# A four-layer hybrid kernel on one core: convolution pieces and the first step size issued ahead of the rest of the projection, and an L1 gate product that reads PSUM

## The chip, the core and the metric

The kernel is one program on one core of a Trainium2 chip. The engines named below are PE (matrix products, with PEld for its weight loads), DVE (vector), ACT (scalar functions), POOL (GpSimd) and SP, whose queue issues every DMA of this kernel. Each engine works through its own list of instructions in order. SBUF is the on-chip memory, PSUM the eight banks that PE writes to and that DVE and ACT can also read and write. The metric is device time in microseconds (us); lower is better. Each kernel is run several times and the median is taken, and one further execution is profiled.

## The reference, cut to what matters

The input x is [4, 96, 64, 64] in float32: batch, channels, height, width. Four layers follow; the change touches the first two.

Layer 0 is a selective scan over an image (d_inner 192, 16 states, 4 directions K):

```python
xz = layernorm(t) @ in_proj_w.T + in_proj_b
xi, z = jnp.split(xz, 2, axis=-1)                  # 192 channels each
xi = silu(depthwise_conv3x3(xi) + conv_b)          # per image [192, 64, 64]
xr = xi.reshape(b, 192, L)                         # row by row, L = 4096
xc = xi.transpose(0, 1, 3, 2).reshape(b, 192, L)   # column by column
xs = [xr, xc, flip(xr), flip(xc)]                  # the 4 directions
x_dbl = einsum('bkdl,kcd->bkcl', xs, x_proj_w)     # -> dts_r (6), B (16), C (16)
dt = softplus(einsum('bkrl,kdr->bkdl', dts_r, dt_projs_w) + dt_projs_b)
h = h * exp(dt * A) + dt * B * x ;  y = sum_n h * C   # step by step along L
y  = sum of the 4 directions + Ds * xs ;  layernorm ;  * silu(z) ;  @ out_proj_w.T
```

followed by a residual and a GELU MLP. Layer 1 is a smaller scan (96 channels, one state, 2 directions) whose last part is a layer norm, a gate and a product with a weight:

```python
y = (y - mu) * rsqrt(var + 1e-5)
y = y * out_norm_w + out_norm_b
y = y * silu(z)
out = einsum('oc,bchw->bohw', out_proj_w, y)
```

Layers 2 and 3 (a filter in the Fourier domain, a linear attention and two quantized MLPs) are not touched.

## The kernel before, in words

**A planner sets the order.** The parts of the kernel are Python generators, run as threads by the class `Work`. A thread yields `on(engine, events..., banks=n, took=..., table=...)` when it wants an engine, and the planner picks the thread whose request can start first by its own estimates of costs. The order in which instructions are issued comes out of that, once, when the program is built. Events (`post("rows", ...)`, `("begun",)`, ...) are conditions of this plan; data dependences are guarded apart from them. Lower `rank` wins between equals: the threads of the loop have 0 (`recurs` 2), those of the background 1. `par(jobs, n)` runs a list of jobs on n workers.

**The loop (layer 0's scan).** There are 64 steps, 16 for each batch b: directions k = 0, 1, 3, 2 with 4 chunks of 1024 positions. A step has 24 units (3 blocks j of channels, 4 groups q of states, 2 halves p). `preludes` prepares a step g on 512 columns and 128 partitions: it loads `xi`, multiplies it by `xw` (PE) and copies the result to `xd` (ACT), stores `bc`, then makes three products with `dtw` into banks, of which ACT takes Abs and Relu into `dtu`, then Exp and Ln over all three, then POOL adds and multiplies by `xi`; four puts store `dtu` to `dd` in DRAM. `loads_du` and `loads_bc` bring `u`, `dt`, `bb`, `cc` back, spread over 128 partitions, 512 KB each. For a unit, `decays` computes h = exp(A dt) into PSUM (ACT), `sources` w = u * bb (POOL), `recurs` the scan over h and w and then w = h * cc (DVE), and `gathers` sums w into `py` (PE). One unit in 12 has its last product on POOL (`side`). Buffers: 6 of w (`WB`), 3 of u and of dt (`DB`), 5 of bb and of cc (`RB`). `convolved` loads `xj`, the convolved input that opens a block's sum in direction 0.

**The front of layer 0.** `front(b)` has two phases. In `inproj(gp)`, four jobs that each take column group gp of both image halves: x is loaded and normalized, then multiplied by `w_in` three times: into `xp01` (channels 0 to 127, padded image), `xp2` (channels 128 to 191, the two image halves on two halves of the partitions), and `z`, of which ACT takes Silu before it is stored to `z_d`. Then come the convolutions: `conv(q)` for part 1 (from `xp2`, 4 pieces of 8 rows) and afterwards for part 0 (from `xp01`, 8 pieces), with three workers. A piece is 9 products with diagonal weights on PE, into a bank; for the first batch two pieces of each part are instead nine multiply-adds on DVE (`taps`), into the SBUF tile `xi` itself. ACT then takes Silu; POOL copies the piece, transposed, to `xt`; SP stores it to `xi_d`. After a part, `xt` is stored too: 2 puts for part 0, 16 for part 1, whose runs are 128 bytes.

**The start.** The program first runs `setup()` and `front(0)` with all eight banks (3 of `bm`, 5 of `bs`; `mode["wide"]`), until the event `("inproj", 0)`. Then the five `bs` banks are given to h and py, and the threads of the loop start; the convolutions of batch 0 run as background of the loop. Pieces of part 0 with q >= 2 wait for `("begun",)`, which step 0 posts after its Ln. After `front(0)` the background goes on with `prepare()` (weights for later layers, by many small loads), `front(1)` to `front(3)`, and `rest(b)` for the four batches: `tail`, `l1`, `l2_front`, `l2_middle`, `back`. A tail's four gates wait for the y of their chunk (`("y", b, c)`, c = 3, 2, 1, 0), which the loop stores as it finishes them in direction 2. When the loop is over, what is left of `rest(3)` runs alone, with eight banks again.

**The L1 gate.** In `l1`, `piece(n)` of the second direction ends with the normalization: `pv` is a bank that holds rsqrt of the variance, `dt` the centred y, `yf` the stored Silu(z). Two DVE instructions form the gated value in `a`, lines 928 to 931.

In the profile, most instructions carry the line of a helper: L227 is `mm` on PE, L242 `act` and L231 `copy` on ACT, L239 a table load of ACT, L254 an operation on DVE or POOL, L275 a load and L279 a store on SP. They are told apart by the names of their tiles.

Of the kernel before, what the change touches and what calls it, by code (L numbers as in the profile page):

```python
# [216 lines left out]
def tile_hybrid(ctx: ExitStack, tc: tile.TileContext, I: dict, out: bass.AP):  # L217
# [238 lines left out]
    def front(b):  # L456
# [3 lines left out]
        dgs = [px_.tile([128, 9, 128], F32, name=f"dg{i}") for i in range(2)]  # L460
        st, (wp, wk) = pools(bg("f1"), bg("f1w"))
# [23 lines left out]
        def inproj(gp):  # L485
            def job(t):
# [47 lines left out]
                ps = yield on("pe", banks=3)  # L534
# [17 lines left out]
        for i in range(2):  # L552
            get(dgs[i], I[("dg01", "dg2")[i]])
        yield from par([inproj(gp) for gp in range(4)], 2, 4)
        st.close()
# [3 lines left out]
        for part in (1, 0):  # L559
            rows = 64 if part == 0 else 32  # L560
            st, (wp, wk) = pools(bg(f"f2{part}"), bg(f"f2w{part}"))
            dg = dgs[part]
            xt = wp.tile([128, 64, rows], F32, name="xt")
            xp = (xp01, xp2)[part]

            def conv(q):
                def job(t):
                    xi = wt(wk, 128, "xi", t)
                    early = b == 0 and (t == 0 if part else q < 2)
                    if b == 0 and part == 0 and q >= 2:  # L570
                        yield on(None, ("begun",))
                    if early:
                        yield from taps(xi, xp, 8 * q, V("cw", j=9 * part, n=9))
                        pc = xi
                    else:
                        (pc,) = yield on("pe", banks=1)
                    for k in () if early else range(9):
                        kh, kw = divmod(k, 3)
                        r = 8 * q + kh
                        mm(  # L580
                            pc.rearrange("p (h w) -> p h w", w=WW), lhsT=dg[:, k, :],
                            rhs=xp[:, r : r + 8, kw : kw + 64], start=(k == 0), stop=(k == 8),
                        )
                        if k in (2, 5):
                            yield on("pe")
                    yield on("act", took=0.7, table=AF.Silu)
                    act(xi, pc, AF.Silu, bias=V("cb", j=part))
                    if not early:
                        drop(pc)
                    yield on("pool")  # L590
                    po_.tensor_copy(
                        xt[:, :, 8 * q : 8 * q + 8], xi.rearrange("p (h w) -> p w h", w=WW)
                    )
                    yield on("sp")
                    if part == 0:
                        put(xi_d[b][0, q, 0:128], xi)
                        post("rows", b, q, stored=True)
                    else:
                        for h in range(2):
                            put(xi_d[b][0, q + 4 * h, 128:192], xi[64 * h : 64 * h + 64])  # L600

                return job

            yield from par([conv(q) for q in range(rows // 8)], 3)
            if part == 1:
                post("half", b)
            yield on("sp")
            if part == 0:
                v = xi_d[b][1, :, 0:128, :].rearrange("g d t -> d g t")
                xf = xt.rearrange("p (g w) h -> p g (w h)", g=NG)  # L610
                for i in range(2):
                    put(v[:, 4 * i : 4 * i + 4], xf[:, 4 * i : 4 * i + 4])
            else:
                v = xi_d[b][1, :, 128:192, :].rearrange("g d (w h) -> d g w h", h=HH)
                for h in range(2):
                    for g in range(NG):
                        put(v[:, g, :, 32 * h : 32 * h + 32], xt[64 * h : 64 * h + 64, 8 * g : 8 * g + 8, :])
            st.close()
# [117 lines left out]
    def l1(b, stat, pp, big):  # L736
# [112 lines left out]
        def piece(n):  # L849
# [4 lines left out]
            def job(t):  # L854
# [73 lines left out]
                ve.scalar_tensor_tensor(a, dt, V("l1og", C), pv[0:C], ALU.mult, ALU.mult)  # L928
                drop(pv)
                yield on("dve")  # L930
                ve.scalar_tensor_tensor(a, a, V("l1ob", C), yf, ALU.add, ALU.mult)
# [431 lines left out]

    def preludes():
        ck, dp = fg["ck"], fg["dp"]
        for g, (b, k, s, c) in enumerate(steps):
            need = [("front", b)] if k % 2 else [("half", b), ("rows", b, 2 * c), ("rows", b, 2 * c + 1)]
# [29 lines left out]
            for j in range(3):  # L1397
                (pd,) = yield on("pe", banks=1)
                mm(pd, lhsT=dtw[:, j, :], rhs=xd[0:64], start=True, stop=True)
                yield on("act", took=1.3)  # L1400
                act(dtu[:, 0, j], pd, AF.Abs)
                act(dtu[:, 1, j], pd, AF.Relu)
                drop(pd)
            yield on("act", took=1.6, table=LN_EXP)
            act(dtu[:, 0], dtu[:, 0], AF.Exp, scale=-1.0)
            yield on("act", took=1.6, table=LN_EXP)
            act(dtu[:, 0], dtu[:, 0], AF.Ln, bias=one)
            if g == 0:
                post("begun")
            yield on("pool")  # L1410
            po_.tensor_add(dtu[:, 0], dtu[:, 0], dtu[:, 1])
            yield on("pool")
            po_.tensor_mul(dtu[:, 1], dtu[:, 0], xi)
            yield on("sp")
            dd = dp.tile([2, 3, 2, 32, 2, HC], F32, tag="dd", name="dd")
            for p in range(2):
                for hf in range(2):
                    r = p * 64 + hf * 32
                    put(
                        dd[:, :, p, :, hf, :].rearrange("t j d i -> d (t j) i"),  # L1420
                        dtu[r : r + 32].rearrange("d t j i -> d (t j) i"),
                    )
            sync()
            d["dd"] = dd
            post("dd", g)

    def loads_du():

        for n in range(6 * NS_):
            g, m = divmod(n, 6)  # L1430
            for t in (1, 0):
                need = [("dd", g)]
# [13 lines left out]
    def loads_bc():  # L1446

        for n in range(4 * NS_):
            g, q = divmod(n, 4)
            for t in range(2):  # L1450
                need = [("bc", g)]
                if n >= RB:
                    o, r = divmod(n - RB, 4)
                    need.append(("src" if t == 0 else "C", unit(o, 2, r, 1)))
                yield on("sp", *need)
                tag = ("bb", "cc")[t]
                x = fg["ring"].tile([128, CH], F32, tag=tag, name=tag)
                r = t * NS + 4 * q
                get(x, made[g]["bc"][r : r + 4].unsqueeze(0).to_broadcast([32, 4, CH]))
                made[g][tag, q] = x  # L1460
                post(tag, n)
                wk_.detach()
# [108 lines left out]
    def convolved():  # L1571

        was = None
        for block in range(3 * NS_):
# [4 lines left out]
            yield on("sp", ("half", b), ("rows", b, 2 * c + 1), ("bc", g), *([("xjf", was)] if was is not None else []))  # L1579
# [40 lines left out]
    with tc.manual_schedule():  # L1620
        stb = open_banks(3, "bm")
        st = open_banks(5, "bs")
        mode["wide"] = True
        first = wk_.add(setup()), wk_.add(front(0))
        wk_.run(lambda: first[0].done and ("inproj", 0) in wk_.events)
# [3 lines left out]
        st_sb, (ck, du, ring, wk, yp_, dp) = pools(  # L1629
# [192 lines left out]
```

## Time and profile before

Three runs took 6655.88, 6654.35 and 6673.25 us, median 6655.88. The profiled execution took 6648.81 us, of which 6647.0 lie between its first and last instruction (the span).

| stretch of the span, us | length | DVE busy | ACT busy | POOL busy | PE busy | what runs |
|---|---|---|---|---|---|---|
| 0 to 133.3 | 133.3 | 37.08 | 50.75 | 19.27 | 92.22 | setup, front(0), first prelude |
| 133.3 to 218 | 84.7 | 80.38 | 49.68 | 67.89 | 62.35 | step 0 |
| 218 to 251 | 33.0 | 17.24 | 10.78 | 18.43 | 13.49 | the passage to step 1 |
| 251 to 400 | 149.0 | 145.50 | 97.89 | 118.34 | 106.50 | steps 1 and 2 |
| 400 to 2000 | 1600.0 | 1469.15 | 1010.52 | 1277.86 | 1294.82 | loop, fronts, first rest |
| 2000 to 4000 | 2000.0 | 1887.86 | 1320.53 | 1592.93 | 1612.26 | loop and rests |
| 4000 to 5980 | 1980.0 | 1872.27 | 1402.35 | 1582.79 | 1576.59 | loop and rests |
| 6100 to 6647 | 547.0 | 198.82 | 288.81 | 0.00 | 435.42 | rest(3) alone |

The last scan of the loop starts at 6079.30. "Busy" is time in which the engine executes an instruction, waits inside the instruction included. A timeline row gives start, duration, engine, line, operation, output and inputs, their shapes, and in brackets how long the engine was idle before it and what released it. A group row gives the busy sum and mean duration, then the idle time ahead of the group. In the stretch 40 to 55.4 the z part shows as twelve Silu activations of 0.69 us on ACT (the first at 43.35, the last at 54.68) and sixteen puts on SP that begin at 44.06 and take 12.91 us together.

### The profile page before, as it was taken

The numbers are of one execution on the slowest core, as the hardware profiler recorded it, in microseconds if no ns is written. First come the engines' busy times: TensorE is split into PE (matmuls) and PEld (weight loads), VectorE is DVE, ScalarE is ACT, GpSimd is POOL, SyncE is SP. The second block draws the span as 40 slices with busy tenths as digits, with TensorE's granted clock in tenths as the row PEclk, the third lists the DMA queues.
The fourth block names the chain that finished last, engine by engine and source line by source line (L and its number), as shares of the span: only waits on it lengthen the run. The fifth ranks groups of instructions, "written<-read, shape, count | busy, mean of one in ns | idle before, by whom it ended". The sixth has DMA issues, their size and how long they took to land. (4 is left out here: it accounts for less than half of the span.)

```text
span 6647.0 us, 55955 instructions
## 1 busy us (share of the span) xinstructions
PE 5289.4 (80%) x15752; PEld 1653.6 (25%) x15752; DVE 5807.2 (87%) x3872; ACT 4308.0 (65%) x6520; POOL 4740.5 (71%) x2148
## 2 busy tenths in 40 slices
PE   7678888977867888767777888877777888877788
PEld 2122221222211332212211232212211232212273
DVE  4898989899989999999989999999989999996613
ACT  4565756666766557876666567887666567885636
POOL 2778787787798787787698687787698687883000
PEclk8689999978879999888778999889778999888778
DMA  5656566565555685555555585555565586552451
GB/s 146 191 169 193 164 187 189 166 196 182 174 181 163 214 283 174 168 188 177 161 183 163 186 295 186 165 185 186 164 183 163 182 294 186 169 178 76 154 158 34
DMA packets 532384, 1189.24 MB, mean 179 GB/s; under 512 B 90158, under 2 KB 163451, under 8 KB 532060
## 3 DMA queue, kind: packets, MB, share of 16 engines
q1 hardware_dynamic: 532072, 1185.66, 57.0%
q8 instruction: 125, 2.05, 0.1%
q14 instruction: 187, 1.53, 0.1%
HBM read 937.80 MB, written 247.63 MB: 178 GB/s over the span
## 5 line engine op out<-in xcount | busy, mean ns | idle before, releaser
L254 POOL TENSOR_TENSOR w<-u,bb 128x1024 f32<-128x1024 f32 x1536 | 3607.6, 2374 | 907.0 <-PE py L227 785.3
L254 DVE TENSOR_TENSOR_SCAN h<-h,state,w 128x1024 f32<-128x1024 f32 x1056 | 2480.8, 2349 | 177.5 <-ACT h L242 89.2
L227 PE MATMUL py<-w,sel 128*32 128x512 f32 x6144 | 1847.9, 930 | 511.3 <-DVE w L254 381.7
L242 ACT ACTIVATE h<-dt,negA 128x1024 f32<-128x1024 f32 x1536 | 1727.7, 1125 | 428.5 <-DVE w L254 304.1
L254 DVE TENSOR_TENSOR w<-h,cc 128x1024 f32<-128x1024 f32 x1408 | 1721.8, 1223 | 109.5 <-DVE h L254 3.2
L254 DVE TENSOR_TENSOR_SCAN h<-h,w 128x1024 f32<-128x1024 f32 x352 | 805.5, 2288 | 112.7 <-POOL w L254 60.0
L231 ACT COPY state<-h 128x1 f32<-128x1 f32 x1056 | 166.2, 157 | 762.7 <-DVE w L254 761.1
L227 PEld LDWEIGHTS py<-w,sel 128*32 128x32 f32 x6144 | 188.0, 114 | 1595.7 <-DVE w L254 962.2
L254 POOL TENSOR_TENSOR w<-w,cc 128x1024 f32<-128x1024 f32 x128 | 301.9, 2358 | 165.6 <-ACT state L231 92.9
L227 PE MATMUL bm<-xp,dg 128*128 128x512 f32 x792 | 372.1, 616 | 0.9 <-ACT dtu L242 0.9
L227 PE MATMUL bm<-xi,xw 128*128 128x512 f32 x384 | 225.3, 733 | 99.8 <-DMA xi<-xi_d 84.6
L254 POOL TENSOR_TENSOR dtu<-dtu 128x1536 f32<-128x1536 f32 x64 | 221.3, 3458 | 84.7 <-ACT dtu L242 49.7
L242 ACT ACTIVATE dtu<-bm 128x512 f32<-128x512 f32 x384 | 209.0, 599 | 65.5 <-PE bm L227 62.8
L227 PE MATMUL bm<-xd,dtw 64*128 64x512 f32 x384 | 218.8, 654 | 21.8 <-ACT xd L242 9.9
L254 DVE TENSOR_TENSOR_SCAN w<-h,state,w 128x1024 f32<-128x1024 f32 x96 | 224.8, 2342 | 2.9 <-ACT h L242 2.7
L254 POOL TENSOR_TENSOR dtu<-dtu,xi 128x1536 f32<-128x1536 f32 x64 | 220.9, 3452 | 3.9
L227 PEld LDWEIGHTS bm<-xp,dg 128*128 128x128 f32 x792 | 148.5, 195 | 281.8 <-issue 263.0
L227 PE MATMUL bm<-big,dg 96*96 96x512 f32 x432 | 208.6, 625 | 10.8 <-ACT u L242 7.6
L227 PE MATMUL py<-Y,eye 128*128 128x512 f32 x288 | 166.2, 660 | 42.6 <-ACT Y L231 39.8
L242 ACT ACTIVATE bm<-bm,eps 96x512 f32<-96x512 f32 (+1 forms) x210 | 135.7, 646 | 64.7 <-PE bm L227 64.4
L242 ACT ACT_TABLE_LOAD x119 | 152.7, 1283 | 20.7 <-PE bm L227 18.7
L227 PE MATMUL bm<-x,cent 96*96 96x512 f32 x278 | 148.9, 628 | 19.6 <-DMA x<-in_x 5.5
(317 smaller groups left out, 6994.6 us busy)
## 6 DMA issues: line engine op xcount, KB each, us to landing
u<-dd SPq DMA_DIRECT2D x384, 512.0 KB
dt<-dd SPq DMA_DIRECT2D x384, 512.0 KB
bb<-bc SPq DMA_DIRECT2D x256, 512.0 KB
cc<-bc SPq DMA_DIRECT2D x256, 512.0 KB
dd<-dtu SPq DMA_DIRECT2D x256, 384.0 KB
xi<-xi_d SPq DMA_DIRECT2D x256, 192.0 KB
f_d<-fo SPq DMA_DIRECT2D x64, 384.0 KB
a<-f_d SPq DMA_DIRECT2D x64, 384.0 KB
```

The costliest lines, as they stand in the source:

```text
L227: return nc.tensor.matmul(o, lhsT=lhsT, rhs=rhs, **kw)
L231: return nc.scalar.copy(o, i, **kw)
L242: return nc.scalar.activation(o, i, func, **kw)
L254: return f(o, *a, **kw)
```

## The change

It has four parts.

1. **Order of the front of batch 0.** The convolutions become one job list over (part, q), with two workers in place of three, one pool for both parts, and the store ahead of the transposing copy. In batch 0, four pieces, (0,0), (0,1), (1,0), (1,1), are added as a thread before the projection jobs start; each waits for the `("xp", b, gp)` events of the column groups that it reads. The first three are taps on DVE, with a bank as their accumulator instead of `xi`; (1,1) runs on PE and posts `("ez",)`. The projection jobs of batch 0 wait for `("ez",)` before their z products. The other eight pieces follow as background, part 1 first; in batch 0 those with q >= 2, of either part, wait for `("begun",)`. All 18 puts of the transposed tiles come at the end.
2. **Step 0 in thirds.** For g = 0, the dt products, Abs and Relu, Exp, Ln, the two POOL passes and the four puts are issued for one j at a time (512 columns instead of 1536, 12 puts instead of 4), and `loads_du` waits for its third alone. `("begun",)` is posted after the third Ln. The loads of bb and cc for q = 1 to 3 of step 0, and `convolved`, wait for `("dt", 1)`.
3. **`preludes` starts in the first phase.** Its pools are opened ahead; it waits for the four pieces that its chunk needs (`rows_of`) instead of `("half", b)` and two rows. The first phase ends when, in addition, no `bs` bank is held.
4. **The L1 gate.** The first product writes to `pv`, the second reads it there.

```diff
+        ahead_ = b == 0
+        if ahead_:
+            stc, (xtp, ck) = pools(bg("f2"), bg("f2w"))
+            xts = [xtp.tile([128, 64, rows], F32, name=f"xt{rows}") for rows in (64, 32)]
...
-                ps = yield on("pe", banks=3)
+                post("xp", b, gp)
+                ps = yield on("pe", *([("ez",)] if ahead_ else []), banks=3)
...
+        def conv(part, q):
+            dg, xt, xp = dgs[part], xts[part], (xp01, xp2)[part]
+
+            def job(t):
+                xi = wt(ck, 128, "xi", t)
+                if b == 0 and q >= 2:
+                    yield on(None, ("begun",))
+                near = [("xp", b, v) for v in {q % 4, (q + 1) % 4, max(q - 1, 0) % 4, *((3,) if part and q == 0 else ())}]
+                early = ahead_ and (part, q) in ((0, 0), (0, 1), (1, 0))
+                (pc,) = yield on("dve" if early else "pe", *near, banks=1)
+                if early:
+                    yield from taps(pc, xp, 8 * q, V("cw", j=9 * part, n=9))
...
+                if (part, q) == (1, 1):
+                    post("ez")
...
+                post("rows", b, part, q, stored=True)
...
+        order = [(0, 0), (0, 1), (1, 0), (1, 1)] if ahead_ else []
+        if ahead_:
+            soon = wk_.add(par([conv(p, q) for p, q in order], 2))
         yield from par([inproj(gp) for gp in range(4)], 2, 4)
+        if ahead_:
+            yield on(None, lambda: soon.end if soon.done else None)
...
-            yield from par([conv(q) for q in range(rows // 8)], 3)
...
+        rest_ = [(p, q) for p in (1, 0) for q in range(8 - 4 * p) if (p, q) not in order]
+        yield from par([conv(p, q) for p, q in rest_], 2)
...
-                ve.scalar_tensor_tensor(a, dt, V("l1og", C), pv[0:C], ALU.mult, ALU.mult)
+                ve.scalar_tensor_tensor(pv[0:C], dt, V("l1og", C), pv[0:C], ALU.mult, ALU.mult)
+                yield on("dve")
+                ve.scalar_tensor_tensor(a, pv[0:C], V("l1ob", C), yf, ALU.add, ALU.mult)
                 drop(pv)
-                yield on("dve")
-                ve.scalar_tensor_tensor(a, a, V("l1ob", C), yf, ALU.add, ALU.mult)
...
+    def rows_of(b, c):
+
+        return [("rows", b, 0, 2 * c + i) for i in range(2)] + [("rows", b, 1, (2 * c + i) % 4) for i in range(2)]
...
-            need = [("front", b)] if k % 2 else [("half", b), ("rows", b, 2 * c), ("rows", b, 2 * c + 1)]
+            need = [("front", b)] if k % 2 else rows_of(b, c)
...
+            for j0, j1 in ((0, 1), (1, 2), (2, 3)) if g == 0 else ((0, 3),):
+                js = slice(j0, j1)
+                for j in range(j0, j1):
+                    (pd,) = yield on("pe", banks=1)
...
+                if g == 0 and j1 == 3:
+                    post("begun")
...
+                for j in range(j0, j1):
+                    post("dd", g, j, stored=True)
...
-                need = [("dd", g)]
+                need = [("dd", g, m // 2)]
...
-                need = [("bc", g)]
+                need = [("bc", g), *([("dt", 1)] if 1 <= n < 4 else [])]
...
+        ts = [wk_.add(preludes(), 0)]
-        wk_.run(lambda: first[0].done and ("inproj", 0) in wk_.events)
+        wk_.run(
+            lambda: first[0].done and ("inproj", 0) in wk_.events
+            and not any(k.startswith("bs") for k in wk_.held.values())
+        )
```

## The prediction

> **What bounds the kernel now.** I read the page first: engine totals, then the slices of the span.
>
> ```profile
> PE 5289.4 (80%) x15752; PEld 1653.6 (25%) x15752; DVE 5807.2 (87%) x3872; ACT 4308.0 (65%) x6520; POOL 4740.5 (71%) x2148
> ...
> DVE  4898989899989999999989999999989999996613
> ```
>
> VectorE (DVE) is full in almost every slice except the first and the last three. Between lies a loop of 1536 units, each one scan (2.29 to 2.35 us) and, in 11 of 12, one product (1.22 us). So two things count: when the first scan starts, and anything that adds time to DVE inside the loop. The background (fronts 1 to 3 and the four rests) feeds on the loop's results: every tail waits for the last y chunk of its batch and ends 88 to 100 us after it (b=0: chunk stored at 1606, last x1 row at 1694; b=1: 3088 and 3188; b=2: 4589 and 4687). An earlier loop therefore carries the end with it.
>
> Next the timeline, engine by engine, before the first scan. Columns: start, duration, instruction, idle time and its releaser.
>
> ```profile
> 78.59 10.49 DVE L254 SCALAR_TENSOR_TENSOR xi<-xp,vec,xi 128x512 f32<-128x512 f32 x14
> 133.33 2.30 DVE L254 TENSOR_TENSOR_SCAN h<-h,w 128x1024 f32<-128x1024 f32 x1 [44.26 <-POOL w L254]
> ...
> 102.88 0.69 ACT L242 ACTIVATE xd<-bm,vec 128x512 f32<-128x512 f32 x1 [13.05 <-PE bm L227]
> 104.78 3.18 ACT L242 ACTIVATE dtu<-bm 128x512 f32<-128x512 f32 x6 [1.21 <-PE bm L227]
> 109.27 1.48 ACT L242 ACTIVATE dtu<-dtu 128x1536 f32<-128x1536 f32 x1
> 110.79 1.57 ACT L242 ACTIVATE dtu<-dtu,one 128x1536 f32<-128x1536 f32 x1
> ...
> 112.44 3.42 POOL L254 TENSOR_TENSOR dtu<-dtu 128x1536 f32<-128x1536 f32 x1 [20.29 <-ACT dtu L242]
> 115.94 3.43 POOL L254 TENSOR_TENSOR dtu<-dtu,xi 128x1536 f32<-128x1536 f32 x1
> ...
> 119.40 4.21 SPq L279 DMA_DIRECT2D dd<-dtu  x4
> 124.94 0.64 SPq L275 DMA_DIRECT2D u<-dd  x1
> ```
>
> DVE stands idle 44.26 us: this is a latency chain with one thing at a time in it. Four tap pieces end at 89.1; the last Silu ends at 89.83; xi is loaded from 91.74; PE starts at 97.56, cold (5.28 us for six passes); then xd, the three dt products, Exp and Ln on 1536 columns, two POOL passes, four puts; u arrives at 130.89, POOL needs 2.35 more.
>
> Third, the DVE groups: first inside the loop (400 to 6081), then after it, where POOL does nothing; last, the DVE and POOL timelines around one case.
>
> ```profile
> L254 DVE SCALAR_TENSOR_TENSOR a<-a,vec,cc 96x512 f32<-96x512 f32 x24 | 67.5, 2816 | 1.7 <-DMA cc<-z_d 1.7
> ...
> L254 DVE SCALAR_TENSOR_TENSOR a<-a,vec,cc 96x512 f32<-96x512 f32 x8 | 6.0, 748 | 0.3
> ...
> 1979.88 4.30 DVE L254 SCALAR_TENSOR_TENSOR a<-a,vec,cc 96x512 f32<-96x512 f32 x1
> ...
> 1979.00 2.34 POOL L254 TENSOR_TENSOR w<-w,cc 128x1024 f32<-128x1024 f32 x1
> 1981.30 2.34 POOL L254 TENSOR_TENSOR w<-u,bb 128x1024 f32<-128x1024 f32 x1
> ```
>
> The same instruction takes 748 ns alone and 2816 ns in the loop. At 1979.88 it ends at 1984.18: POOL's second product ends at 1983.64, and 0.75 before 1984.18 is 1983.4. It did nothing until POOL paused. It reads two SBUF tensors (a and cc).
>
> **The L1 gate.** The first product now writes to pv (PSUM), so the second reads pv and one SBUF tensor. Nearest row, in the same loop: a<-dt,vec,bm, one SBUF and one PSUM input, 725 ns mean and never over 743. So 67.5 - 24 x 0.725 = 50.1 us leave DVE; the 8 pairs after the loop gain nothing. Writing to PSUM: scans that write h (PSUM) take 2349 ns, those that write w (SBUF) 2342, so no cost. [...] The rows show waits over two and three products (up to 7.98 us), so I take 50. [...] The rows have 725 with PSUM and 748 without; I take nothing. Does the saving reach the end? In 3500 to 3700 DVE is busy 192.4 of 200 us and POOL 159.2; in 5000 to 5180 DVE 174.3 and POOL 142.2 of 180. In 1900 to 2160 POOL has 237.2 of 260 and may bind next. Ends 20 and 50; I take 85%, **43 us**. pv's bank is held for one more product of 0.7 us plus its turn on DVE: hidden by the other two banks, a few us of background if not.
>
> **The start.** Three pieces of taps instead of four run on DVE, right after their input. The first needs column groups 0 and 1 of xp; ACT ends those at 40.1. 27 taps at 0.75 (14 in 10.49) are 20.3: 60.5. Group 3's rows, needed by (1,0), end at 49.7 even with the z Silus (12 x 0.69) between, which now come later. Silu 0.7: 61.3. To the xi load 1.9, to PE 5.8, as now: 69.0. Projection 2.7 instead of 5.3 if PE is warm (the same six passes at 162.68 took 2.74): 71.7. xd 0.7; one product and its evacuation 1.2 + 1.1: 74.8. Table load 1.28; Exp and Ln on 512 columns 0.6 each: 77.3. POOL a third of 6.85: 79.6. Four puts of a third: between 1.4 and 4.2, taken 2.3; 1.3 to the u load; 5.95 until it lands (bb and cc of q 1 to 3 are queued behind dt 1 now, so perhaps 4); 2.35 on POOL: **91.6**. What is moved into this stretch is the whole z part: 12 Silus (8.3 us of ACT), their products, and 16 puts that held SP for 12.9 us, in the same queues as the xi load, bc and dd. Between 0 and 10 us late; I take 3: 94.6, and 133.3 - 94.6 = **39 us**. The other two thirds are due only at units 8 and 16, 29 and 58 us later, and their 8 extra puts lie beside the loop. xj and bb/cc of q=1 wait for dt 1; the w ring of six covers this.
>
> **What is late next.** Step 1 needs rows of (0,2), (0,3), (1,2), (1,3). All wait for "begun", which now comes about at the first scan instead of 21 us ahead (112.36). In the loop a convolution piece takes some 12.5 us (Silus at 126.9 and 177.0 with four pieces between): rows about 55 us after the first scan, dd some 45 later (it took 57, from 142.4 to 199.6, with three workers on the three banks; now one bank stays free), u and w 8 more: 108, against 86 when step 0 ends. A stall of about 19. Before, this boundary already stalls:
>
> ```profile
> 229.59 2.36 DVE L254 TENSOR_TENSOR_SCAN h<-h,state,w 128x1024 f32<-128x1024 f32 x1 [12.22 <-ACT state L231]
> ```
>
> with 2.84 and 0.99 after it, 16 in all, because u was issued only at 221.69, behind the small weight loads of prepare, although dd was out at 199.6. These come later now. Ends -16 and +20; I take 3 us lost.
>
> Front(0) ends later: eight pieces after the start and all 18 transposed puts, about 215 instead of 184. Fronts 1 to 3 follow without a gap, the last ending at 1335, just as y(0,3) is stored at 1329. So rest(0) starts about 70 us late against its chunks. rest(1) and rest(2) already start 73 and 91 late, and their tails end 100 and 98 behind the last chunk instead of 88: about 12 us there, some **5** at the end.
>
> **Sum.** 43 + 39 - 3 - 5 = 74. The profiled execution took 6648.8 (span 6647.0), so 6575; the median of the runs lies 7 higher, so 6582, and I say 6580.
>
> **Rivals.** What a measurement can tell is 0.3%, 20 us.
> - *Forecast*, both parts hold: 6550 to 6610, chance 0.57.
> - *POOL binds next* in the L1 stretches: waits on POOL's w there were up to 2.5 us (3467). The gate brings 15 to 20 instead of 43: 6605. For it the 91% POOL of 1900 to 2160; against it the 80% of the others. 0.16.
> - *The head start is eaten at step 1*: the stall grows to 16 + 39 and only the gate is left: 6656 - 43 = 6613, with more lag in the background up to 6640. For it, four pieces in front of the second xi load instead of two. 0.13.
> - *Slower: the fronts.* Two convolution workers instead of three. A phase of 12 pieces took 412 to 614, 200 us. If workers set its pace it takes 300, three times; with 30 from front(0), rest(0) starts at 1670 and not 1341. A tail at its own pace takes 300 us (2888 to 3188), so beyond some 100 us late everything passes on: rest(3) would start near 6130, after the loop, and its 744 us (5903 to 6647), shortened to some 600 without the loop beside it, end near 6730. It decides from about 40 us more per phase. Against it: 12 PE chunks in 424 to 475, one in 4.3 us, which looks like the pace of PE, and the barrier between the two parts (478 to 496) is gone. 0.09.
> - *No difference*, the planner's new order costing what the parts bring: DVE idles some 370 us in the loop for many small reasons. 0.05.
>
> So faster 0.85, same 0.06, slower 0.09; the range 6545 to 6635.
>
> **What would show it.** First scan at 90 to 100; DVE's longest wait before it about 30 us, not 44; the second gate product at 0.72 us in the loop, never above 0.8; a wait of 5 to 35 us at the start of step 1; rest(0) starting near 1341 to 1390. I am wrong if the first scan comes after 110, if the gate product still shows waits of several us, if DVE's waits on POOL's w grow by over 20 us in the L1 stretches, or if the last xi_d put of front(3) comes after 1420.

## The result, and the profile after

Five runs of the changed kernel took 6578.41 to 6604.20 us, median 6591.18, against 6662.19 for the kernel before beside it: ratio 0.9893 with the interval 0.9878 to 0.9908, so 71 us or 1.1% faster. A second set of four runs of the same program gave a median of 6584.74 (0.9874, interval 0.9858 to 0.9891). The profiled execution took 6589.22 us, 59.6 less than the profiled one before. That pair differs less than the medians because the execution profiled before lies below its own runs: 6648.81, with a median of 6662.19.

The page of after, engine totals and slices:

```profile
PE 5261.5 (80%) x15770; PEld 1657.9 (25%) x15770; DVE 5753.2 (87%) x3863; ACT 4317.5 (66%) x6528; POOL 4740.2 (72%) x2152
...
DVE  5799999999988999999889999999989999996613
```

DVE's busy time fell by 54.0 us, about what the gate removes. Its share stays at 87% because the span shrank too. The first slice rises from 4 to 5, because the loop begins earlier. The second falls from 8 to 7: there step 1 now waits longer. The fourth, sixth and eighth rise from 8 to 9.

The start, from the timelines of DVE, ACT, POOL and SP:

```profile
52.44 6.30 DVE L254 SCALAR_TENSOR_TENSOR bs<-xp,vec,bs 128x512 f32<-128x512 f32 x8
93.23 2.30 DVE L254 TENSOR_TENSOR_SCAN h<-h,w 128x1024 f32<-128x1024 f32 x1 [34.50 <-DMA u<-dd]
...
74.98 0.69 ACT L242 ACTIVATE xd<-bs,vec 128x512 f32<-128x512 f32 x1 [4.85 <-PE bs L227]
79.28 0.63 ACT L242 ACTIVATE dtu<-dtu 128x512 f32<-128x512 f32 x1
79.94 0.72 ACT L242 ACTIVATE dtu<-dtu,one 128x512 f32<-128x512 f32 x1
...
80.74 1.27 POOL L254 TENSOR_TENSOR dtu<-dtu 128x512 f32<-128x512 f32 x1 [19.09 <-ACT dtu L242]
90.53 2.34 POOL L254 TENSOR_TENSOR w<-u,bb 128x1024 f32<-128x1024 f32 x1 [4.62 <-DMA u<-dd]
...
83.38 1.74 SPq L279 DMA_DIRECT2D dd<-dtu  x4
86.19 0.52 SPq L275 DMA_DIRECT2D u<-dd  x1
```

The chain is the same as before, with its links shorter: Exp and Ln 0.63 and 0.72 instead of 1.48 and 1.57, POOL 1.27 instead of 3.42, four puts in 1.74 instead of 4.21. The first scan starts at 93.23, 40.1 us earlier.

The gate, groups of DVE inside the loop (400 to 6021):

```profile
L254 DVE SCALAR_TENSOR_TENSOR a<-bm,vec,cc 96x512 f32<-96x512 f32 x24 | 17.5, 734 | 1.0 <-DMA cc<-z_d 1.0
L254 DVE SCALAR_TENSOR_TENSOR bm<-dt,vec,bm 96x512 f32<-96x512 f32 x24 | 17.5, 734 | 0.4 <-ACT bm L242 0.4
```

2816 ns became 734: 24 x 2.082 = 50.0 us. The first product, which now writes to PSUM, takes 734 where it took 724.

The passage to step 1, DVE's timeline, first the two waits of before that follow its 12.22:

```profile
236.05 2.36 DVE L254 TENSOR_TENSOR_SCAN h<-h,state,w 128x1024 f32<-128x1024 f32 x1 [2.84 <-ACT state L231]
...
240.67 2.36 DVE L254 TENSOR_TENSOR_SCAN h<-h,state,w 128x1024 f32<-128x1024 f32 x1 [0.99 <-POOL w L254]
```

and then after:

```profile
204.28 2.36 DVE L254 TENSOR_TENSOR_SCAN h<-h,state,w 128x1024 f32<-128x1024 f32 x1 [25.33 <-ACT state L231]
...
212.09 2.36 DVE L254 TENSOR_TENSOR_SCAN h<-h,state,w 128x1024 f32<-128x1024 f32 x1 [0.54 <-POOL w L254]
...
234.32 2.36 DVE L254 TENSOR_TENSOR_SCAN h<-h,state,w 128x1024 f32<-128x1024 f32 x1 [4.21 <-ACT state L231]
...
251.66 2.36 DVE L254 TENSOR_TENSOR_SCAN h<-h,state,w 128x1024 f32<-128x1024 f32 x1 [8.77 <-ACT h L242]
...
255.93 2.36 DVE L254 TENSOR_TENSOR_SCAN h<-h,state,w 128x1024 f32<-128x1024 f32 x1 [0.65 <-ACT h L242]
```

39.5 us of waiting, where it was 12.22 + 2.84 + 0.99 = 16.05. So 23.4 of the 40.1 us were gone by 260. What came after that is read from the stores of y, where y(b,c) is chunk c of batch b: y(0,3) is 35.6 us earlier than before (1293.1, was 1328.7), so 19 us came back between 260 and 1293. The three stretches with an L1 (from y(b,0) to the next batch's y(b+1,3)) are shorter by 0.4, 13.8 and 15.3, the four stretches from y(b,3) to the last y of their batch longer by 6.7 in all; the last y is 58.4 earlier. From the last scan of the loop (6020.9) to the end it takes 566.5 us, where it took 567.7.

### The profile page after: what moved, and what is told of

Its sections match the earlier page's. It is cut to its first block, busy times and chain, and to the rows that moved or that the text cites. A ratio compares the mean times of both kernels' runs of the same rounds, so it can differ in the third digit from the quotient of the medians.

```text
span 6587.4 us, 55972 instructions
## 1 busy us (share of the span) xinstructions
PE 5261.5 (80%) x15770; PEld 1657.9 (25%) x15770; DVE 5753.2 (87%) x3863; ACT 4317.5 (66%) x6528; POOL 4740.2 (72%) x2152
## 5 line engine op out<-in xcount | busy, mean ns | idle before, releaser
L227 PE MATMUL py<-w,sel 128*32 128x512 f32 x6144 | 1796.2, 933 | 496.5 <-DVE w L254 332.1
L254 POOL TENSOR_TENSOR dtu<-dtu 128x1536 f32<-128x1536 f32 (+1 forms) x66 | 221.7, 3358 | 103.0 <-ACT dtu L242 55.4
L227 PE MATMUL bm<-xd,dtw 64*128 64x512 f32 x382 | 223.8, 670 | 21.1 <-ACT xd L242 11.3
L254 POOL TENSOR_TENSOR dtu<-dtu,xi 128x1536 f32<-128x1536 f32 (+1 forms) x66 | 221.5, 3356 | 3.9
L227 PE MATMUL bm<-big,dg 96*96 96x512 f32 x432 | 208.5, 625 | 11.4 <-ACT u L242 7.6
L227 PE MATMUL py<-Y,eye 128*128 128x512 f32 x288 | 166.2, 660 | 44.4 <-ACT Y L231 35.6
```

The lines of the kernel that those rows point to most:

```text
L227: return nc.tensor.matmul(o, lhsT=lhsT, rhs=rhs, **kw)
L254: return f(o, *a, **kw)
```

## The experiments

Medians in us, of 4 to 6 runs, and ratios to the kernel before run beside them. The four marks are read in each kernel's one profiled execution: its first scan, the first scan of step 1, the store of y(0,3), the last store of y. Where one program was profiled twice (after, split loads), the first three marks differ by up to 3.8 us and the last by up to 9.6, so differences of that size say little.

| kernel | first scan | step 1 | y(0,3) | last y | median | ratio, interval |
|---|---|---|---|---|---|---|
| before | 133.3 | 229.6 | 1328.7 | 5995.8 | 6662.2 | 1 |
| after | 93.2 | 204.3 | 1293.1 | 5937.3 | 6591.2 | 0.9893 (0.9878 to 0.9908) |
| after, again | 94.3 | 204.7 | 1296.9 | 5932.6 | 6584.7 | 0.9874 (0.9858 to 0.9891) |
| gate alone | 134.4 | 230.3 | 1333.0 | 5976.5 | 6622.2 | 0.9936 (0.9923 to 0.9949) |
| start alone | 94.7 | 205.2 | 1297.5 | 5972.6 | 6626.5 | 0.9947 (0.9933 to 0.9961) |
| xj not held back | 94.7 | 252.3 | 1335.2 | 5952.9 | 6603.4 | 0.9913 (0.9898 to 0.9928) |
| split loads | 93.9 | 204.4 | 1287.8 | 5918.9 | 6578.7 | 0.9872 (0.9857 to 0.9887) |
| split loads, again | 91.2 | 203.6 | 1284.4 | 5928.5 | 6578.5 | 0.9867 (0.9852 to 0.9882) |
| step 0 whole | 104.7 | 201.9 | 1280.2 | 5917.4 | 6569.6 | 0.9859 (0.9845 to 0.9873) |
| taps for (0,2), (0,3) | 93.0 | 202.7 | 1298.4 | 5933.2 | 6579.0 | 0.9875 (0.9860 to 0.9890) |
| begun at the first third | 91.3 | 201.0 | 1291.2 | 5919.0 | 6594.3 | 0.9887 (0.9869 to 0.9904) |
| whole, with the taps | 107.0 | 191.2 | 1300.1 | 5941.1 | 6597.9 | 0.9898 (0.9883 to 0.9913) |
| old fronts 1 to 3 | 92.1 | 203.3 | 1309.3 | 5938.0 | 6592.7 | 0.9894 (0.9880 to 0.9908) |
| whole and split loads | 105.6 | 202.9 | 1283.2 | 5917.3 | 6567.2 | 0.9855 (0.9842 to 0.9869) |

### The two halves of the change

The gate edit alone, put into the kernel before; and the changed kernel with the gate as before.

```diff
-                ve.scalar_tensor_tensor(a, dt, V("l1og", C), pv[0:C], ALU.mult, ALU.mult)
+                ve.scalar_tensor_tensor(pv[0:C], dt, V("l1og", C), pv[0:C], ALU.mult, ALU.mult)
...
-                ve.scalar_tensor_tensor(a, a, V("l1ob", C), yf, ALU.add, ALU.mult)
+                ve.scalar_tensor_tensor(a, pv[0:C], V("l1ob", C), yf, ALU.add, ALU.mult)
```

> The kernel before with the new L1 gate alone. Theory (the gate frees 50 us of VectorE, of which the loop keeps 85%): 43 us less than before, ratio 0.9935, and the second gate product at 0.72 to 0.75 us everywhere. Rival (another wait takes its place, as the spacing of the stored y chunks in the changed kernel hints: it won 0, 14 and 14 us in the three batches): 20 to 28 us less, ratio 0.996 to 0.997. First scan at 133, as before, in both.

> The changed kernel with the old L1 gate. First scan at 93 as in the changed kernel. If the gate is worth 43 us, this is 71 - 43 = 28 us below before (ratio 0.996); if it is worth 25, this is 46 us below (ratio 0.993). The gate product should again take up to 8 us in the loop. If the two parts add, its gain and that of the gate alone sum to 71.

The gate is worth 42 us (the interval: 34 to 51), the rest of the change 37 (26 to 45). Their sum, 79, is within the spread of the 71 measured together. The single profiles of the gate alone and of before differ by 19.6 only. In them the three L1 stretches shrink by 1.4, 14.7 and 14.6, where the rows lost 8 x 1.27 = 10.2, 19.6 and 20.2: 31 of 50 us kept, against 42 by the medians. The first stretch falls short of its 10.2 in all twelve profiles with the new gate (0.2 to 6.1). In the gate alone DVE's waits for ACT's h grow there from 20.5 to 25.4 us and those for POOL's w from 7.2 to 7.5 (1610 to 2820): part of the freed time became waits for ACT. Why this happens there and less in the other two stays open.

### What sets step 1: xj, the loads of prepare

In after, PE waits 15.24 us for `xj` between 83 and 98 with the convolutions queued behind:

```profile
98.22 2.05 PE L227 MATMUL py<-xj,diagD 128*128 128x512 f32 x2 [15.24 <-DMA xj<-xi_d]
```

So `convolved` was freed of its wait for `("dt", 1)`.

```diff
-            yield on("sp", *rows_of(b, c), ("bc", g), ("dt", 1), *([("xjf", was)] if was is not None else []))
+            yield on("sp", *rows_of(b, c), ("bc", g), *([("xjf", was)] if was is not None else []))
```

> The changed kernel, but the xj loads of step 0 do not wait for dt 1. In the changed kernel PE stood idle for 15.2 us (83 to 98) with the product of xj at the head of its queue and convolution pieces behind it. Theory (this held up the pieces that step 1 needs): their first Silu moves from 110 to about 96, the wait at the start of step 1 falls from 25.3 us to 10 to 15, and the time by 10 to 15 us. Rival (the pieces are paced by ACT's table loads and by PE in the loop, or dd of step 1 by something else): the wait stays above 20 us and the time within 5 us of the changed kernel.

That fell: no gain, rather 12 to 19 us lost, by the two medians of after. The earlier xj changed the planner's order. Timelines of SP and DVE of this kernel:

```profile
204.74 15.12 SPq L279 DMA_DIRECT2D xi_d<-xt  x18
219.96 4.47 SPq L279 DMA_DIRECT2D dd<-dtu  x4
...
252.25 2.36 DVE L254 TENSOR_TENSOR_SCAN h<-h,state,w 128x1024 f32<-128x1024 f32 x1 [20.24 <-POOL w L254]
```

The puts of dt now stand behind the 18 transposed puts, and the `u` loads behind the loads of `prepare`: step 1 starts 48 us later than in after. Yet the last y is only 15.6 later. By these two profiles about a third of the loss reached that point.

The second edit splits the loads of 97 rows, `bn` and `wkv`, into 96 and 1.

```diff
-        get(bn, I["bn1"].partition_broadcast(C + 1))
+        get(bn[0:C], I["bn1"].partition_broadcast(C))
+        get(bn[C : C + 1], I["bn1"].partition_broadcast(1))
...
-        get(wkv, I["l3_wkv"])
+        get(wkv[0:C], I["l3_wkv"][0:C])
+        get(wkv[C : C + 1], I["l3_wkv"][C : C + 1])
```

> The changed kernel, with two loads of prepare over 97 partitions split into 96 and 1. In the changed kernel the load of bn (291 KB) took about 15 us, and SP waited 8.2 us for it before the load eight places later, with dt of step 1 behind. Theory ([...] each DMA waits for the one eight places ahead): bn lands in 2 to 5 us, the 8.2 us wait goes, and with it the waits of VectorE of 4.2 and 8.8 us at 234 and 252: 8 to 13 us less. Rival (the small-element loads beside it are what is slow): the wait on SP moves to another load and the time stays.

> The changed kernel with thirds and the two loads of 97 rows split, a second time, beside the whole step: 6579 within 6 us if the gain of 12 us over the changed kernel is real; 6585 to 6591 if it was the spread of the runs. In the trace SP's wait of 8 us inside the loads and DVE's 8.8 us wait for dt behind it are gone in either case.

SP's timeline in after:

```profile
226.86 0.32 SPq L275 DMA_DIRECT2D bn<-in_bn  x1
...
233.27 0.46 SPq L275 DMA_DIRECT2D gam<-in_bn  x1
241.85 0.31 SPq L275 DMA_DIRECT2D prep<-in_l_w2T  x1
...
246.53 0.59 SPq L275 DMA_DIRECT2D dt<-dd  x1
```

and the longest of SP's waits from 220 to 262 (source, sum, times, longest):

```profile
SPq L275 <- DMA bn<-in_bn: 8.1, 1, 8.1
```

Between `gam` and `w2T` SP stands still for 8.1 us, and this wait names `bn`. `w2T` is the eighth DMA after it. It is so in before too, where SP waits 8.2 us for `bn` (203.09) ahead of `w2T` (219.00): here a DMA waits for the one eight places ahead. The `dt` that step 1 needs is queued behind. With the loads split, SP and DVE:

```profile
232.69 0.42 SPq L275 DMA_DIRECT2D gam<-in_bn  x1
233.15 0.42 SPq L275 DMA_DIRECT2D prep<-in_l_w2T  x1
...
237.11 0.59 SPq L275 DMA_DIRECT2D dt<-dd  x1
...
243.79 2.36 DVE L254 TENSOR_TENSOR_SCAN h<-h,state,w 128x1024 f32<-128x1024 f32 x1 [0.67 <-ACT h L242]
```

dt is issued 9.4 us earlier, and DVE's 8.77 became 0.67. Other waits grew a little, so that from the end of step 0 to 262 DVE waits 33.1 and 30.3 us in the two profiles with split loads, where both of after have 39.5 and 39.3. The medians are 12.5 below the first and 6 below the second set of after, and two sets with the split agree (6578.7, 6578.5). The trace shows SP's wait gone, which rules out that the loads beside `bn` were the slow ones; for the time, the intervals overlap those of after.

### What the thirds bring

Step 0 whole again, all else as changed:

```diff
-            for j0, j1 in ((0, 1), (1, 2), (2, 3)) if g == 0 else ((0, 3),):
+            for j0, j1 in ((0, 3),):
```

> The changed kernel with step 0 whole again: dt over all 1536 columns at once, four puts, u waits for all of it; everything else as after the change. Theory: the pieces ahead of the projection bring most of the 40 us by which the first scan came earlier, and the thirds bring what a third of the passes saves. Whole, after the second dt product, Abs and Relu of three products (6 x 0.55), Exp and Ln over 1536 columns (1.5 + 1.6 instead of 0.63 + 0.72), two POOL passes of 3.4 instead of 1.27 (+4.3), and puts of three times the bytes: first scan about 10 to 14 us later, at 103 to 108. How much of it reaches the end depends on what a late start costs: if the step-1 boundary only waits for dt of step 1, which depends on the convolution of (0,3), the boundary wait shrinks by as much and the time rises by 3 or less (6588 to 6596 on 6591); rival: all of it counts, 6601 to 6606.

The first scan comes 11.4 us later than in after, as expected. But the kernel is not slower: 6569.6 beside 6584.7. Timelines of PE and DVE with the whole step:

```profile
77.44 18.30 PE L227 MATMUL bm<-xp,dg 128*128 128x512 f32 x42
...
104.67 2.30 DVE L254 TENSOR_TENSOR_SCAN h<-h,w 128x1024 f32<-128x1024 f32 x1 [46.88 <-POOL w L254]
...
201.87 2.36 DVE L254 TENSOR_TENSOR_SCAN h<-h,state,w 128x1024 f32<-128x1024 f32 x1 [10.64 <-POOL w L254]
...
250.05 2.36 DVE L254 TENSOR_TENSOR_SCAN h<-h,state,w 128x1024 f32<-128x1024 f32 x1 [3.84 <-ACT h L242]
```

Step 1 begins at 201.87, before the 204.28 of after: it waits for its own dt, which is ready at about 200 in both, so the 11 us are paid back in the wait. More than that is won. From the end of step 0 to 262 DVE waits 15.6 us in place of 39.5. The stretch 93 to 262 of after and of the whole step (window, length, busy time of PE, PEld, DVE, ACT and POOL with their instructions, granted clock, DMA share, GB/s):

```profile
93.00:262.00 169.00, 116.91 (x324) 38.90 (x324) 122.97 (x72) 86.74 (x124) 113.83 (x54) 0.81 0.57 181
```

```profile
93.00:262.00 169.00, 116.09 (x311) 35.31 (x309) 134.25 (x78) 85.65 (x122) 124.91 (x57) 0.78 0.65 200
```

DVE gets 11.3 us more work done, and this lead lasts: y(0,3) comes 13 to 17 us earlier than in the two profiles of after and the last y 15 to 20, and the median is 15 below that of the second set of after, run beside it. Part of it is DVE's wait of 8.77, which becomes 3.84; that the order of SP's queue brings this is the author's estimate.

In the time from 77 to 96 PE does 42 products of convolution here and 6 in after, since `("begun",)` comes with the Ln at 81.7 instead of 97.7. Two edits tried whether that late event is what costs: `("begun",)` after the first third, and, with the event left where it is, (0,2) and (0,3) as taps in DVE's idle 34 us.

```diff
-                if g == 0 and j1 == 3:
+                if g == 0 and j1 == 1:
                     post("begun")
```

> The changed kernel with the event begun posted after the Ln of the first third instead of the third, so that the remaining convolution pieces may be planned from there on. Observed: with thirds the event comes with the third Ln (97.7), with step 0 whole at 81.7; PE then does 42 products of convolution between 77 and 96 with the whole step and 6 with thirds, and the whole step ends 15 us faster although its first scan is 11 later. Theory: it is the late event that takes back what the thirds bring. With the event at about 80 PE is filled between 79 and 98, the xi load of step 1 goes at about 135 or earlier instead of 145, the wait at the start of step 1 falls from 25 to 15 or less, and the time is 6566 to 6576 on 6585 to 6591, as with the whole step. Rival: the thirds' own cost (their 12 puts and the wait of bb and cc for the second third) or the chain from xi to u (59 us in both) sets step 1: the wait stays over 20 and the time within 6 of 6588.

```diff
+                late = ahead_ and (part, q) in ((0, 2), (0, 3))
-                if b == 0 and q >= 2:
+                if b == 0 and q >= 2 and not late:
                     yield on(None, ("begun",))
...
-                (pc,) = yield on("dve" if early else "pe", *near, banks=1)
-                if early:
+                if late:
+                    pc = xi
+                else:
+                    (pc,) = yield on("dve" if early else "pe", *near, banks=1)
+                if early or late:
                     yield from taps(pc, xp, 8 * q, V("cw", j=9 * part, n=9))
+                if late:
+                    yield on(None, ("begun",))
...
+        if ahead_:
+            rest_.sort(key=lambda v: (v not in ((0, 2), (0, 3)), -v[0], v[1]))
```

> The changed kernel with pieces (0,2) and (0,3) as nine multiply-adds each on DVE into their SBUF tile, ahead of the first scan, where DVE idles 34.5 us (58.7 to 93.2); their Silu still waits for the third Ln, and (1,2), (1,3) follow on PE. Theory: the 25 us wait at the start of step 1 comes from the chain (0,3) Silu 144.1, load of xi at 145.2, product at 157, dt at 182 to 189, u at 201.8; with these pieces off PE the xi load can go at about 125, so u of step 1 lands about 20 us earlier and the wait falls from 25 to 5 us or less. Time 6591 - 15 to 20 = 6571 to 6576. Rival: the chain waits for its turn behind the foreground's products on PE and not for the pieces, then the wait stays at 20 or more and the time within 6 of 6591. Second rival: what the loop gains at the boundary it loses later, because the background did its work in that wait: y(0,3) gains less than half of what the boundary gains.

The early event does fill PE, with 36 products of convolution between 74 and 93. But in both kernels the wait at step 1 stays:

```profile
201.04 2.36 DVE L254 TENSOR_TENSOR_SCAN h<-h,state,w 128x1024 f32<-128x1024 f32 x1 [22.96 <-ACT state L231]
```

```profile
202.70 2.36 DVE L254 TENSOR_TENSOR_SCAN h<-h,state,w 128x1024 f32<-128x1024 f32 x1 [23.15 <-ACT state L231]
```

On the wait the rivals held, and the times (6594.3, 6579.0) lie on either side of after's two medians. With the early event the xi load of step 1 went at 138.9, with the taps at 141.2, instead of 145.2, and `u` landed 59.3 and 58.6 us behind it, in after 56.6. Neither the event nor the pieces alone sets step 1. Put together, the whole step and the taps:

> The changed kernel with step 0 whole and with pieces (0,2) and (0,3) as multiply-adds on DVE before the first scan. Theory: what counts is when dt of step 1 is ready, and that is 59 us after its xi load, which waits for (0,2), (0,3), (1,2) and (1,3). Here all four can be done by about 100 and the xi load stands ahead of the second u loads of step 0, at 105 to 115 instead of 140; so u of step 1 lands about 170, before step 0 ends at about 189, and the wait at the start of step 1 (10.6 with the whole step alone) is below 2. The time is then 8 to 10 us under the whole step's 6570: 6559 to 6563. Rival: as with these taps and thirds (6579 against 6585, wait 23), the products of dt wait for their turns among the foreground's on PE, so that the wait stays above 7 and the time is within 5 of 6570.

The first half of the theory held: the xi load goes at 120.6, and step 1 starts right after step 0. DVE's timeline:

```profile
188.98 2.28 DVE L254 TENSOR_TENSOR_SCAN w<-h,w 128x1024 f32<-128x1024 f32 x1
191.18 2.33 DVE L254 TENSOR_TENSOR_SCAN h<-h,state,w 128x1024 f32<-128x1024 f32 x1
```

The second half fell: 6597.9, no faster than after, and slower than the whole step alone (0.9898 against 0.9859, the intervals apart). DVE was busy 141.4 us between 93 and 262, 18.5 more than in after (123.0), and 25.0 less from 262 to 1290 (941.9 against 967.0). Its waits there, for this kernel (source, sum, times, longest):

```profile
DVE h L254 <- POOL w L254: 25.0, 14, 5.8
DVE h L254 <- ACT h L242: 19.5, 15, 4.1
DVE h L254 <- ACT state L231: 15.3, 9, 8.1
```

and for after:

```profile
DVE h L254 <- ACT h L242: 19.1, 26, 2.3
DVE h L254 <- POOL w L254: 9.6, 5, 2.6
DVE h L254 <- ACT state L231: 4.8, 5, 1.5
```

So the wait was not abolished but moved, into many small waits for POOL and ACT. Which work of the background causes them was not separated.

### Where 19 us came back

After the passage to step 1 the loop gained on the kernel before. The fronts of batches 1 to 3 have a merged list of convolutions too. They were put back: part 1, then part 0, three workers, the copy ahead of the store, the puts after each part.

```diff
+        if not ahead_:
+            for part in (1, 0):
+                rows = (64, 32)[part]
+                stc, (xtp, ck) = pools(bg(f"f2{part}"), bg(f"f2w{part}"))
+                xts = {part: xtp.tile([128, 64, rows], F32, name=f"xt{rows}")}
+                yield from par([conv(part, q) for q in range(rows // 8)], 3)
...
```

> The changed kernel, with the convolutions of batches 1 to 3 as before the change: part 1 first, then part 0, three workers, own pools, the copy ahead of the store, the transposed puts after each part. Batch 0 stays as changed. Observed: after the step-1 boundary only 17 us of the 40 us are left, yet y(0,3) is stored 36 us earlier than before. Theory A: the merged list of the fronts costs the loop less than the two phases did, and gives these 18 us: here y(0,3) comes about 1311 and the time is 6605 to 6612. Theory B: the 18 us are work of front(0) that was done in the boundary's wait and is not in the loop's way later: here nothing changes, y(0,3) within 5 us of 1293 and the time 6585 to 6597. My prediction's slower rival (two workers make the fronts slow) would have this kernel faster than 6591 by 10 or more.

> The changed kernel again, as a baseline on the same chip: 6591 within 6 us, first scan at 93, wait of 25 us at the start of step 1, y(0,3) at 1293 within 3 us.

Busy time of DVE from 262 to 1290 (window, its length, busy, instructions, granted clock, DMA share, GB/s), first of before, then of after, then with the old fronts:

```profile
262.00:1290.00 1028.00, 952.35 (x560) 0.92 0.57 178
```

```profile
262.00:1290.00 1028.00, 966.99 (x573) 0.91 0.60 184
```

```profile
262.00:1290.00 1028.00, 951.99 (x564) 0.92 0.59 180
```

With the old fronts DVE gets in sum what it got before, 15 us less work done than with the merged list (11.7 by the second profile of after, 963.7), and y(0,3) comes at 1309.3, as theory A said. Work done in the wait (theory B) is not the reason. The sums match, the shapes do not: from 1000 to 1290 DVE is busy for 279.5 us in before and 267.3 with the old fronts. Of these 12 to 16 us the last y shows 1 to 5, and the time 8 (6592.7 against 6584.7, the intervals overlap), where theory A had 6605 to 6612: the gain in the loop up to y(0,3) is shown, its arrival at the end is not. Four things were put back together (the order, the three workers, the copy, the puts); which of them counts was not separated.

### A faster version

> The changed kernel with step 0 whole and the two loads of 97 rows split into 96 and 1. Theory, from the whole step (6570 against 6585 in one call) and the split loads (6579 against 6591): the head start of the first scan is not what carries the change, so that the whole step loses nothing against thirds, and the split takes out a wait of 8 to 9 us in step 1 which the whole step has only in part (3.8): 6560 to 6570, at least 5 below the split with thirds run beside it. Rival: the whole step's 15 us were the luck of one plan and one set of runs; then it stands within 6 of the split with thirds, or above it.

The whole step with split loads took 6567.2, 11.3 below thirds with split loads run beside it, whose interval overlaps. In two pairs of sets run side by side the whole step was ahead, by 15 and by 11 us. Its interval (0.9842 to 0.9869) lies below that of the first set of after and overlaps the second; it is the fastest version found, 95 us faster than before.

## Why the prediction was right, point by point

The forecast was 6580, with 6545 to 6635; it was 6591 and 6585. Of its four terms two were right and two were not, with opposite signs. That the sum came so near is therefore partly luck: the passage to step 1 cost 20 us more than was put down, and about as much was made good, up to y(0,3) by the fronts, which the sum had at nothing, and at the end by a lag that did not come.

**The gate, 43.** Right. 50.0 us left DVE as reckoned from the rows, and the gate alone brought 42. The rival that POOL binds next is out: POOL's w made DVE wait 34.8 us in the stretches that hold L1 work (1620 to 2300, 3090 to 4310, 4545 to 5810) before, and 38.0 after, 3 us more and not 20. The first of the three stretches, where POOL was busiest, kept least, but there too DVE's waits on POOL's w hardly grew (6.9 and 8.7 us from 1620 to 2300, first before, then after):

```profile
DVE h L254 <- POOL w L254: 6.9, 6, 2.0
```

```profile
DVE h L254 <- POOL w L254: 8.7, 8, 2.0
```

The prediction's lower end of 20 was the author's estimate and no row showed it. A PSUM source shows no cost in these products: 734 ns in the loop and 746 after it, against 748 for the old form after the loop. The taps with a PSUM accumulator take 756 ns, those into SBUF 751 (before, 78.5 to 89.2). Only the first tap of a piece, one input times a weight, pays: 0.75 us into a bank, where it took 0.48 into SBUF, 0.8 us in all.

**The first scan at 94.6.** Right within 1.4 us, by errors that cancel: the taps ended 1.8 us early, at 58.7, but the xi load went at 63.25, as reckoned; PE's six passes took 5.37 and not 2.7, u landed in 4.3 us and not 5.95, and the 3 us kept for the z part were not used by it. Its last put ends at 75.1, ahead of bc at 75.7, and its products end 0.2 us before the passes:

```profile
69.57 5.37 PE L227 MATMUL bs<-xi,xw 128*128 128x512 f32 x6 [0.18 <-issue]
```

The prediction called the 5.28 us of before "cold", the time of a PE that had been idle, there for 27.27 us. Here PE had worked since 59.55, and the passes are as slow. Their time goes with the granted clock of the 4 to 6 us around them: 5.37 us at 0.52 (69 to 75), 5.28 at 0.54 (before, 97 to 103), 2.74 at 1.00 (before, 162 to 166). Time multiplied by clock is 2.7 to 2.9 in all three. What set the clock is not shown.

**The passage to step 1, "I take 3 us lost".** This step failed: 23.4, just beyond the upper end of 20. The chain was reckoned well, w of step 1 coming 108 us after the first scan by the forecast and 111 by the trace; the wait is 25.3 where it said 19. (Its own 108 less 86 gives 22.) The other 14.2 us were missed. The prediction said of prepare's loads that they "come later now". They did, but only behind the first `u` of step 1 and still ahead of its later `dt`: the loads stand at 226 to 245, and the split takes 6 to 9 us of the waits away, those for `bn`. In before the wait for this one load was already 8.2 of the 22 us between dd (out at 199.5) and the `u` of step 1 (221.69); the prediction laid them on the small loads together.

**The background's lag, 5.** It did not appear: from the last scan to the end it takes 1.2 us less than before.

**Not in the sum:** the merged list of the fronts. The slower rival feared that two workers would make the fronts slow. Up to y(0,3) the opposite is shown: front(3)'s last puts start at 1322.7 (forecast: not after 1420), and the old fronts cost the loop 12 to 16 us there. Together with the lag that stayed away this is about the size of what the passage took; how much of it lasts to the end is not shown.

**What the sum assumed without saying:** that a us at the start is a us at the end. It is not. With thirds the first scan comes 11 us earlier and brings nothing, because step 1 starts no earlier; in the one kernel without the wait at step 1 the time is no better; 48 us lost at step 1 cost 15.6 at the last y. The rival "the head start is eaten at step 1" was thus half true. It did not win because step 1 itself also moved, from 229.6 to 204.3, and to 201.9 with step 0 whole, so that the thirds are not what moved it. No run took the pieces ahead of the projection alone; that they, with the prelude in the first phase, carry most of the start's 37 us is inferred from the whole step, which has them without the thirds.

## What to carry to other kernels

When work is pulled forward at the start of a long pipeline, reckon when the *second* stage's inputs are ready: here the 11 us by which the thirds bring the first scan forward were waited for there, and a wait that is removed can come back as many small ones, as with the whole step and the taps: 18.5 us more work done by DVE up to 262, 25.0 less from there to 1290. Compare the same DVE instruction in a stretch where POOL works and in one where it is idle: the gate product took 2816 and 748 ns. Moving one of its two SBUF inputs to PSUM is two changed operands; it then took 734 where POOL works, and that was worth 42 us here. Read the order of a DMA queue across stages: one slow load held what was queued behind it for 8 us here.

## What the runs showed of the hardware

The load of `bn`, 291 KB to 97 partitions, kept its place in the queue for 15.0 us (226.86 to 241.85), 20 GB/s. From 235 to 241, while SP waited for it, the mean busy share of the 16 DMA engines was 0.07 at 27 GB/s, in before 0.08 at 29 GB/s (212 to 217). By an estimate from that share little more than one of the 16 was busy (16 x 0.07 = 1.1). As 96 rows and one it held SP for 0.3 us at most. That the count of 97 makes the load slow was the author's assumption when the loads were split; the runs show that the wait goes with the split, and why it does is not shown.

The runs of one program spread more than its profile suggests: with the event moved to the first third they took 6568.8 to 6601.4 us, with the profiled marks of the start within 3.5 us of after's. So a difference of 10 us between two versions here is not settled by five runs of each, and one profile need not be typical: that of this kernel was its fastest run.
